# The rows of attention scores spread to all partitions through DRAM instead of by products of ones with diagonals

## The chip, the cores and the metric

The kernel runs on one core of one Trainium2 chip. The metric is the device time of one execution in microseconds (us); the time before is the median of three runs. A core has a matrix engine (TensorE, PE in the profile, with its weight loads listed apart as PEld), a vector engine (VectorE, DVE), a scalar engine that also evaluates functions (ScalarE, ACT), a general engine that here only issues DMAs (GpSimd, POOL), and SyncE (SP), which also issues DMAs. Each has its own queue of instructions.

## The reference

Four layers over a graph of 2708 nodes with 512 features, each of the form `x = x + layer(relu(layernorm(x)))`, all in float32. The first three multiply the features by a normalised adjacency matrix and by a weight. The change is in the fourth, cut to what matters:

```python
s_left, s_right = (x @ W_sa) @ a_left, (x @ W_sa) @ a_right
scores = s_left[:, None] + s_right[None, :]
e = where(adj != 0, exp(-leaky_relu(scores, 0.01)), 0)
attn = e / (sum(e, axis=1) + 1e-5)
x_a = attn @ (x @ W_sa)
x_b = adj @ (x @ W_gcnb) + b_gcnb
out = sigmoid(attn_a * x_a + attn_b * x_b)
```

`attn_a` and `attn_b` are gates: sigmoids of one number for each node. The kernel works on the transposed matrix: output nodes are columns, and the nodes that are summed over lie on partitions. So `s_right` is a bias for each partition, and `s_left` is a row that every partition must hold. The kernel divides numerator and denominator by a common factor for each output node, built from the least `s_right` (`srmin`). With m = max(s + srmin, 0.01 (s + srmin)), the two rows are a = m - s and b = m - 0.01 s, and exp(-leaky_relu) becomes the lesser of exp(a - s_right) and exp(b - 0.01 s_right).

## The kernel before

**Tiles.** The 2708 nodes are four quarters (`NQ`) of 677 (`Q`): five tiles of 128 (`KT`) and 37 over. The rests of the four quarters are put together in two tail tiles (tile 20 with 4 x 32, tile 21 with 4 x 5), so there are 22 tiles (`NT`). The 677 columns of a quarter are processed as two pieces of 339 (`U`, `W`), the last of which has one column too many.

**Order of the layers.** The matrix products of layers 0 to 2 and of the gate part of layer 3 are built from sub-products of quarters (L538). For layer 3, `aggregate` does outer products 1, 7, 2, 4, 6 and 5, then calls an epilogue for the first half of the tiles, does outer product 3, and calls the epilogue for the second half (tiles 10 to 21). Hooks put other work into it: `row_scales` hangs on outer product 6, reloads of `h` on 5 and 3.

**The gated epilogue** (`gated`). For each tile there are two halves. A half is a product of 128 x 257 in four steps, each two PE instructions (L200), in one of two banks that also hold the products `pl`, `pm` of the rows. ACT takes the gate from the last column (tanh, L1049), DVE adds the bias to the other 256 (L1058), ACT multiplies by the other gate (L1059), and POOL stores the tile to DRAM (L1060).

**The rows** (`column_rows`). For each quarter, DVE makes seven diagonal matrices from `s_left` (L969), PE multiplies them by ones, so that each partition holds the numbers side by side (L970: 14 instructions, since each float32 product is two), ACT copies them from the bank (L1096, L1101 to L1103), and DVE computes the rows a and b with eight operations (L1107 to L1110). Quarter 0's rows are made between the first four gated tiles of the second half and the others (`gated_and_ready`); those of quarter q+1 at the middle of quarter q (`u == 1`, `b == 0`). The places of the rows are the pool tags s1 and s2 for even quarters, s3 and s4 for odd ones; before the attention these hold operands of outer product 3.

**The attention loop** (from L1191). It runs over quarters, pieces and five blocks: four blocks of five tiles and one of tails. `e_step` works one block ahead: a load of the block of the adjacency matrix, ten exponentials on ACT with the row as input (L1119), and two DVE operations that take the lesser and mask it (L1123, L1124). PE then multiplies the block with `h` (L1202, 40 instructions for a full block), DVE sums it up, and one tile of the output is finished beside it (`attention`). At the end of a piece come the tails' products (L600, L605) and four copies of the sums.

**What sets the order.** Python's order of calls is a priority; a scheduler of the tile framework decides from it the order on every engine's queue when the program is built. Waits follow from the use of tiles, and a tile taken from a pool waits until the readers of the tile that had its place are done.

Of the kernel before, what the change touches and what calls it, by code (L numbers as in the profile page):

```python
# [8 lines left out]
FP = mybir.dt.float32  # L9
AF = mybir.ActivationFunctionType  # L10
ALU = mybir.AluOpType

P = 128
D = 512
NC = D // P
N = 2708
NQ = 4
Q = N // NQ
KT = Q // P
R0 = 32  # L20
R1 = Q - KT * P - R0
U = 2
W = (Q + 1) // U
NF = NQ * KT
NT = NF + 2
R1P = 8
G = NQ * R1P
PAD = R1P - R1
# [9 lines left out]
def gnn_kernel(  # L38
# [20 lines left out]
    nc = tc.nc  # L59

    const = ctx.enter_context(tc.tile_pool(name="const", bufs=1))
# [3 lines left out]
    upool = ctx.enter_context(tc.tile_pool(name="upool", bufs=1))  # L65
    ytp = ctx.enter_context(tc.tile_pool(name="ytp", bufs=1))
    small = ctx.enter_context(tc.tile_pool(name="small", bufs=2))
    dram = ctx.enter_context(tc.tile_pool(name="dram", bufs=1, space=bass.MemoryType.DRAM))
    ps_agg = ctx.enter_context(tc.tile_pool(name="ps_agg", bufs=5, space=bass.MemoryType.PSUM))
    ps_out = ctx.enter_context(tc.tile_pool(name="ps_out", bufs=2, space=bass.MemoryType.PSUM))  # L70
# [3 lines left out]
    ident = const.tile([P, P], FP, name="ident")  # L74
# [6 lines left out]
    for k in range(1, P // G):  # L81
# [6 lines left out]
    bab = const.tile([P, 2], FP, name="bab")  # L88
    nc.gpsimd.dma_start(bab[:, 0:1], ba.partition_broadcast(P))
    nc.gpsimd.dma_start(bab[:, 1:2], bb.partition_broadcast(P))  # L90
    deg = const.tile([P, NT], FP, name="deg")
    dinv = const.tile([P, NT], FP, name="dinv")
    dis = const.tile([P, NT], FP, name="dis")
    hd = const.tile([P, NT, 4], FP, name="hd")
    mv0 = const.tile([P, NT, 2], FP, name="mv0")
    ga = const.tile([P, NT, 2], FP, name="ga")
# [1 line left out]
    eps = const.tile([P, NT], FP, name="eps")  # L98
# [9 lines left out]
        for b in range(2)  # L108
        for u in range(U)
    }  # L110

    h = big.tile([P, NT, D], FP, name="h")

# [850 lines left out]
    def broadcast_columns(po, cs):  # L964

        for s, c in enumerate(cs):
            r = c.shape[0]
            dg = small.tile([P, P], FP, tag="diag", name="dg", bufs=2)
            nc.vector.tensor_scalar(dg[:r, :r], ident[:r, :r], c, None, ALU.mult)  # L969
            nc.tensor.matmul(  # L970
                po[:, s * P : s * P + r], ones[:r, :], dg[:r, :r], start=True, stop=True
            )
# [99 lines left out]
    srmin = const.tile([P, 1], FP, name="srmin")  # L1072

    def row_scales():

        mn = small.tile([P, 1], FP, tag="ge", name="mn")
        nc.vector.tensor_reduce(mn, hd[:, :, 1], mybir.AxisListType.X, ALU.min)
        po = ps_out.tile([P, D], FP, tag="out", name="pm")
        broadcast_columns(po, [mn[:, 0:1]])
        nc.vector.tensor_reduce(srmin, po[:, 0:P], mybir.AxisListType.X, ALU.min)  # L1080
        nc.vector.tensor_scalar(nsr[:, :, 0], hd[:, :, 1], -1.0, None, ALU.mult)
        nc.vector.tensor_scalar(nsr[:, :, 1], hd[:, :, 1], -0.01, None, ALU.mult)
        nc.vector.tensor_scalar(eps, hd[:, :, 0], srmin, None, ALU.add)
        nc.vector.scalar_tensor_tensor(eps, eps, 0.01, eps, ALU.mult, ALU.max)
        nc.scalar.activation(eps, eps, AF.Exp)
        nc.vector.tensor_scalar(eps, eps, 1e-5, None, ALU.mult)

    def column_rows(q):

        ra, rb = (  # L1090
            spool.tile([P, U * W], FP, tag=f"s{1 + k + 2 * (q % 2)}", name=f"r{k}") for k in (0, 1)
        )
        nc.vector.memset(ra[:, Q : U * W], 0.0)
        pl = ps_out.tile([P, D], FP, tag="out", name="pl")
        broadcast_columns(pl, [hd[:, q * KT + k, 0:1] for k in range(4)])
        nc.scalar.copy(ra[:, 0 : 4 * P], pl)  # L1096
        pl = ps_out.tile([P, D], FP, tag="out", name="pl")
        broadcast_columns(
            pl, [hd[:, q * KT + 4, 0:1], hd[:, NF, 0:1], hd[:G, NF + 1, 0:1]]
        )  # L1100
        nc.scalar.copy(ra[:, 4 * P : 5 * P], pl[:, 0:P])  # L1101
        nc.scalar.copy(ra[:, KT * P : KT * P + R0], pl[:, P + q * R0 : P + (q + 1) * R0])
        nc.scalar.copy(ra[:, KT * P + R0 : Q], pl[:, 2 * P + q * R1P + PAD : 2 * P + (q + 1) * R1P])  # L1103
        for u in range(U):
            a, b = ra[:, u * W : (u + 1) * W], rb[:, u * W : (u + 1) * W]
            lm = upool.tile([P, W], FP, tag="s", name="lm")
            nc.vector.tensor_scalar(lm, a, srmin, None, ALU.add)  # L1107
            nc.vector.scalar_tensor_tensor(lm, lm, 0.01, lm, ALU.mult, ALU.max)
            nc.vector.scalar_tensor_tensor(b, a, -0.01, lm, ALU.mult, ALU.add)
            nc.vector.tensor_sub(a, lm, a)  # L1110
        return ra, rb

    def scores(blk, ts, ra, rb):
# [62 lines left out]
    def gated_and_ready(ts):  # L1176

        nonlocal ready
        if ts[0] < half:
            return gated(ts)  # L1180
        gated(ts[:4])
        lines[0] = column_rows(0)
        gated(ts[4:])
        ready = e_step(*steps[0])
# [6 lines left out]
    for n, (q, u, b) in enumerate(steps):  # L1191
        cu = slice(u * W, (u + 1) * W)
        se = sums[:, (q % 2) * U * W : (q % 2 + 1) * U * W]
        if b == 0:
            pe = [ps_agg.tile([P, W], FP, tag="agg", name=f"pe{c}") for c in range(NC)]
            if u == 1 and q + 1 < NQ:
                lines[q + 1] = column_rows(q + 1)
# [10 lines left out]
        for t, a in now:  # L1208
            if t == 0:
                nc.vector.tensor_copy(se[:, cu], a)  # L1210
            else:
                r = G if t == NF + 1 else P
# [14 lines left out]
        elif todo:  # L1227
            t, se_t = todo.pop(0)
# [70 lines left out]
```

## Time and profile before

| | |
|---|---|
| median of three runs | 2099.44 us (2096.2 to 2100.52) |
| profiled execution, its own time | 2098.61 us |
| its span, first to last instruction | 2096.7 us |
| granted PE clock | 0.997 of full |
| busy: PE / DVE / ACT / POOL | 2054.8 / 1416.4 / 409.2 / 182.8 us |
| PE instructions of L970 for the rows (`pl`) | 56, from 1580.9 to 1901.9 us |
| gated epilogue of the second half begins | 1567.07 us |
| middles of quarters 0, 1, 2 | 1661.6, 1779.9, 1898.3 us |

A line of the groups names source line, engine, operation, output and inputs with shapes, count, then busy time and mean in ns, then idle time of the engine ahead of it and what ended it. A line of a timeline gives start, duration, engine, line and operation; a number in brackets is the idle time before it and its releaser. Times are from the start of the span. A busy sum counts each instruction with its whole duration, and neighbours overlap; how often one can follow the other is read from their starts.

### The profile page before, as it was taken

Reading aid. Unit: us, or ns where it says so; the run is one execution under the profiler, and the core shown is the slowest. Engines: PE = TensorE matmul, PEld = TensorE weight load, DVE = VectorE, ACT = ScalarE, POOL = GpSimd, SP = SyncE. Lnnn points to the kernel's source line nnn. Section 1 sums busy time; section 2 is a strip of 40 time slices with the busy share of each in tenths; the row PEclk is TensorE's granted clock in tenths of the full one; section 3 lists DMA queues with packets and bytes.
Section 4 is the critical chain, followed back from the end, with each engine's and each line's share of the span. In section 5 each row is a group of like instructions: output and inputs, shape, how many; then the busy total and the mean of one; then the engine's idle time right before and its main releaser. Section 6 shows DMA issues by size and latency. Waiting matters only on the chain.

```text
span 2096.7 us, 20100 instructions
## 1 busy us (share of the span) xinstructions
PE 2054.8 (98%) x7340; PEld 1279.6 (61%) x7340; DVE 1416.4 (68%) x2481; ACT 409.2 (20%) x833; POOL 182.8 (9%) x330
## 2 busy tenths in 40 slices
PE   5999999999999999999999999999999999999998
PEld 2566655656666554666665556666777666666665
DVE  4578877657767777766686889867538755666512
ACT  1430001130000011100002120000117533444411
POOL 0110111120000012000002120000001000000011
PEclk9999999999999999999999999999999999999999
DMA  9998594555545354654445574555451223233220
GB/s 368 302 373 260 188 342 171 188 190 170 175 154 186 126 189 136 242 174 161 166 145 175 195 244 164 169 166 183 153 176 59 101 99 117 81 103 102 90 74 26
DMA packets 79746, 360.86 MB, mean 172 GB/s; under 512 B 10668, under 2 KB 15660, under 8 KB 79520
## 3 DMA queue, kind: packets, MB, share of 16 engines
q1 hardware_dynamic: 50672, 245.43, 34.0%
q0 software_dynamic: 28976, 114.15, 16.8%
q8 instruction: 58, 0.95, 0.2%
q14 instruction: 40, 0.33, 0.0%
HBM read 294.61 MB, written 62.15 MB: 170 GB/s over the span
## 4 chain that ended last, share of the span: by engine, by line
PE 87%; DVE 6%; DMA 4%; issue 1%; ACT 1%; POOL 0%; SPq 0%; POOLq 0%; DVEq 0%; ACTq 0%
PE pe L1202 17%; PE po L200 15%; PE pc L538 14%; PE pd L538 14%; PE pa L538 13%; PE pb L538 7%; PE pt L600 3%; DMA obuf<-in_yb_dram 2%; DMA ends<-in_yt_dram 1%; PE pt L605 1%; PE pe L600 1%; DVE ends L1001 1%; DMA ends<-xs 1%; PE dg_ps L321 1%; DVE t L511 0%
## 5 line engine op out<-in xcount | busy, mean ns | idle before, releaser
L1202 PE MATMUL pe<-obuf,h 128*128 128x339 f32 x1280 | 373.2, 448 | 0.0
L200 PE MATMUL po<-ends,agg 128*128 128x512 f32 (+2 forms) x968 | 352.1, 521 | 1.3 <-DVE ends L1058 1.0
L538 PE MATMUL pa<-obuf,h 128*128 128x339 f32 x1040 | 317.1, 449 | 2.5 <-ACT h L252 1.4
L1202 PEld LDWEIGHTS pe<-obuf,h 128*128 128x128 f32 x1280 | 240.8, 189 | 127.1 <-issue 10.8
L200 PEld LDWEIGHTS po<-ends,agg 128*128 128x128 f32 x968 | 181.3, 190 | 154.3 <-issue 137.4
L538 PEld LDWEIGHTS pa<-obuf,h 128*128 128x128 f32 x1040 | 195.6, 190 | 110.0 <-issue 9.8
L1119 ACT ACTIVATE e<-r,nsr 128x339 f32<-128x339 f32 x352 | 170.9, 565 | 25.0 <-DVE obuf L1123 11.5
L538 PE MATMUL pb<-t,s 128*128 128x339 f32 x560 | 171.2, 452 | 1.8 <-DVE s L470 1.0
L538 PE MATMUL pc<-t,h 128*128 128x339 f32 x560 | 169.5, 448 | 2.1 <-DVE u L585 2.1
L538 PE MATMUL pd<-t,s 128*128 128x339 f32 x560 | 169.0, 448 | 0.0
L538 PE MATMUL pd<-obuf,s 128*128 128x339 f32 x550 | 166.5, 448 | 1.3 <-DVE s L554 0.9
L572 ACT COPY v<-pa 128x339 f32<-128x339 f32 x56 | 24.6, 439 | 724.7 <-PE pa L538 698.8
L538 PEld LDWEIGHTS pb<-t,s 128*128 128x128 f32 x560 | 106.2, 190 | 57.2 <-DVE t L510 2.1
L538 PEld LDWEIGHTS pc<-t,h 128*128 128x128 f32 x560 | 105.7, 189 | 57.3 <-DVE u L585 3.6
L538 PEld LDWEIGHTS pd<-t,s 128*128 128x128 f32 x560 | 105.8, 189 | 54.1
L538 PEld LDWEIGHTS pd<-obuf,s 128*128 128x128 f32 x550 | 104.0, 189 | 55.2 <-DVE s L554 1.5
L538 PE MATMUL pc<-obuf,s 128*128 128x339 f32 x450 | 136.0, 448 | 0.0
L538 PEld LDWEIGHTS pc<-obuf,s 128*128 128x128 f32 x450 | 85.1, 189 | 43.8 <-issue 0.5
L510 DVE TENSOR_TENSOR t<-obuf,t 128x1695 f32<-128x1695 f32 x55 | 105.5, 1918 | 0.0
L932 POOL DMA_DIRECT2D xs<-ends x66 | 35.9, 544 | 782.4 <-DVE ends L931 706.8
L1219 DVE COPY agg<-pe 128x339 f32<-128x339 f32 x16 | 7.5, 507 | 137.0 <-PE pe L605 137.0
L578 DVE TENSOR_TENSOR u<-v,pb 128x339 f32<-128x339 f32 x56 | 28.4, 507 | 106.1 <-PE pb L538 106.0
(273 smaller groups left out, 2225.9 us busy)
## 6 DMA issues: line engine op xcount, KB each, us to landing
obuf<-in_yb_dram SPq DMA_DIRECT2D x132, 847.5 KB, 4.6
obuf<-osumt SPq DMA_DIRECT2D x100, 847.5 KB, 4.5
osumt<-obuf POOLq DMA_DIRECT2D x22, 847.5 KB, 12.2
xs<-ends POOLq DMA_DIRECT2D x66, 256.0 KB, 2.3
ends<-xs POOLq DMA_DIRECT2D x61, 256.0 KB, 3.9
obuf<-in_yt_dram SPq DMA_DIRECT2D x28, 339.0 KB, 3.5
obuf<-in_yb_dram POOLq DMA_DIRECT2D x11, 847.5 KB, 10.8
ends<-in_yb_dram SPq DMA_DIRECT2D x9, 847.5 KB, 9.5
```

Source lines behind the costliest of these rows:

```text
L200: nc.tensor.matmul(po, cs[c], ws[c], start=(c == 0), stop=(c == NC - 1))
L321: nc.tensor.matmul(ps[g], first, y, start=n < 4, stop=n >= len(ops) - 4)
L510: nc.vector.tensor_add(t2, o22, t1)
L538: last = nc.tensor.matmul(ps, x[:, k, :], y[:, k, :], start=start and k == 0, stop=k == KT - 1, skip_group_check=not start,)
L572: at_v.append(nc.scalar.copy(v, pa).ins)
L578: at_u2.append(nc.vector.tensor_add(u2, v, pb).ins)
L600: nc.tensor.matmul(ps[c], h[:, NF, c * P : (c + 1) * P], tl[:, 0, :], start=start, stop=False)
L605: nc.tensor.matmul(ps[c], h[g, NF + 1, c * P : (c + 1) * P], tl[g, 1, :], start=False, stop=True)
L932: nc.gpsimd.dma_start(xs[t], xt)
L1001: nc.vector.tensor_tensor_reduce(y, h[:, t, :], vs[:, k, :], 1.0, 0.0, ALU.mult, ALU.add, hd[:, t, k : k + 1])
L1119: nc.scalar.activation(e[:, k], row, AF.Exp, bias=nsr[:, t, s : s + 1], scale=1.0)
L1202: nc.tensor.matmul(pe[c], h[:, t, c * P : (c + 1) * P], a, start=(t == 0), stop=False)
```

## The change

The rows a and b are computed once for all nodes in `row_scales`, where the numbers lie as 128 x 22: two more DVE operations, which write into `dinv` and `dis` (no longer needed there). `deg`, `dinv` and `dis` become slices of one tile `dd`, so that one product with the identity turns both to 44 x 128. ACT copies that to a tile in SBUF, and 12 DMAs of POOL write it to a DRAM tile `ab_rows`, in the order of the columns (8 of five rows of 128, 2 for the tails of 32, 2 for those of 5). `column_rows` then only clears the last column of each row and loads it with one DMA from POOL's queue, which reads the 677 numbers for every partition (338.5 KB). The places where `column_rows` is called are as before.

```diff
-    deg = const.tile([P, NT], FP, name="deg")
-    dinv = const.tile([P, NT], FP, name="dinv")
-    dis = const.tile([P, NT], FP, name="dis")
+    dd = const.tile([P, 3, NT], FP, name="dd")
+    deg = dd[:, 0]
+    dinv = dd[:, 1]
+    dis = dd[:, 2]
...
+    ab_rows = dram.tile([NQ, 2, U * W], FP, name="ab_rows")
...
         nc.vector.scalar_tensor_tensor(eps, eps, 0.01, eps, ALU.mult, ALU.max)
+        nc.vector.tensor_sub(dinv, eps, hd[:, :, 0])
+        nc.vector.scalar_tensor_tensor(dis, hd[:, :, 0], -0.01, eps, ALU.mult, ALU.add)
         nc.scalar.activation(eps, eps, AF.Exp)
         nc.vector.tensor_scalar(eps, eps, 1e-5, None, ALU.mult)
+
+        po = ps_out.tile([P, D], FP, tag="out", name="pr")
+        nc.tensor.matmul(
+            po[: 2 * NT, 0:P], dd[:, 1:3].rearrange("p k t -> p (k t)"), ident,
+            start=True, stop=True,
+        )
+        r = small.tile([P, P], FP, tag="diag", name="rows", bufs=2)
+        nc.scalar.copy(r[: 2 * NT], po[: 2 * NT, 0:P])
+        for k in range(2):
+            for q in range(NQ):
+                t = k * NT + q * KT
+                nc.gpsimd.dma_start(
+                    ab_rows[q, k, 0 : KT * P].rearrange("(t p) -> t p", p=P), r[t : t + KT]
+                )
+            for o, t, m, c0 in ((KT * P, NF, R0, 0), (KT * P + R0, NF + 1, R1P, PAD)):
+                src = r[k * NT + t : k * NT + t + 1, 0 : NQ * m].rearrange(
+                    "o (q r) -> o q r", q=NQ
+                )
+                nc.gpsimd.dma_start(
+                    ab_rows[:, k, o : o + m - c0].rearrange("(o q) r -> o q r", o=1),
+                    src[:, :, c0:],
+                )
 
     def column_rows(q):
...
-        nc.vector.memset(ra[:, Q : U * W], 0.0)
-        pl = ps_out.tile([P, D], FP, tag="out", name="pl")
-        broadcast_columns(pl, [hd[:, q * KT + k, 0:1] for k in range(4)])
-        nc.scalar.copy(ra[:, 0 : 4 * P], pl)
-        pl = ps_out.tile([P, D], FP, tag="out", name="pl")
-        broadcast_columns(
-            pl, [hd[:, q * KT + 4, 0:1], hd[:, NF, 0:1], hd[:G, NF + 1, 0:1]]
-        )
-        nc.scalar.copy(ra[:, 4 * P : 5 * P], pl[:, 0:P])
-        nc.scalar.copy(ra[:, KT * P : KT * P + R0], pl[:, P + q * R0 : P + (q + 1) * R0])
-        nc.scalar.copy(ra[:, KT * P + R0 : Q], pl[:, 2 * P + q * R1P + PAD : 2 * P + (q + 1) * R1P])
-        for u in range(U):
-            a, b = ra[:, u * W : (u + 1) * W], rb[:, u * W : (u + 1) * W]
-            lm = upool.tile([P, W], FP, tag="s", name="lm")
-            nc.vector.tensor_scalar(lm, a, srmin, None, ALU.add)
-            nc.vector.scalar_tensor_tensor(lm, lm, 0.01, lm, ALU.mult, ALU.max)
-            nc.vector.scalar_tensor_tensor(b, a, -0.01, lm, ALU.mult, ALU.add)
-            nc.vector.tensor_sub(a, lm, a)
+        for k, r in enumerate((ra, rb)):
+            nc.vector.memset(r[:, Q : U * W], 0.0)
+            nc.gpsimd.dma_start(r[:, 0:Q], ab_rows[q, k, 0:Q].partition_broadcast(P))
         return ra, rb
```

## The prediction

> **What bounds the kernel now.** I read the page's busy times first, then the chain that ended last.
>
> ```profile
> PE 2054.8 (98%) x7340; PEld 1279.6 (61%) x7340; DVE 1416.4 (68%) x2481; ACT 409.2 (20%) x833; POOL 182.8 (9%) x330
> PE 87%; DVE 6%; DMA 4%; issue 1%; ACT 1%; POOL 0%; SPq 0%; POOLq 0%; DVEq 0%; ACTq 0%
> ```
>
> TensorE (PE) is busy 98% of the span and carries 87% of the chain. Work of VectorE (DVE) or ScalarE (ACT) that goes away is therefore worth nothing by itself; a product that PE need not do, or a wait of PE, is worth its time. The removed products `pl` (L970) are 56 PE instructions. So I went next to PE's timeline where they stand. At the middle of quarter 0, where the rows of quarter 1 are made:
>
> ```profile
> 1661.58 0.71 PE L970 MATMUL pl<-dg,ones 128*128 128x128 f32 x4
> 1662.13 0.73 PE L1202 MATMUL pe<-obuf,h 128*128 128x339 f32 x2
> 1662.84 0.71 PE L970 MATMUL pl<-dg,ones 128*128 128x128 f32 x4
> 1663.39 0.73 PE L1202 MATMUL pe<-obuf,h 128*128 128x339 f32 x2
> 1663.96 0.61 PE L970 MATMUL pl<-dg,ones 128*128 128x128 f32 x4
> 1664.41 0.73 PE L1202 MATMUL pe<-obuf,h 128*128 128x339 f32 x2
> 1665.07 0.40 PE L970 MATMUL pl<-dg,ones 32*128 32x32 f32 x2
> 1665.41 0.84 PE L1202 MATMUL pe<-obuf,h 128*128 128x339 f32 x2
> ```
>
> From 1661.58 to 1665.41 are 3.83 us, and only six of the block's products stand in them. Ten of those follow each other in 2.86 us elsewhere (1555.64 to 1558.50 in this timeline), 0.286 each, so six need 1.72. The rows cost PE 3.83 - 1.72 = 2.11 us here, gaps included. The same stretch comes again at 1779.94 to 1783.77 and 1898.29 to 1902.12. Quarter 3's middle, at 2016.7, has no rows to make, and PE goes from the tails to the next block without a gap there.
>
> Quarter 0's rows are made inside the gated stretch (lines of PE, then of ACT, then of DVE in the same timeline):
>
> ```profile
> 1567.07 14.04 PE L200 MATMUL po<-ends,agg 128*128 128x257 f32 x64
> 1580.94 0.61 PE L970 MATMUL pl<-dg,ones 128*128 128x128 f32 x4
> 1581.71 2.29 PE L970 MATMUL pl<-dg,ones 128*128 128x128 f32 x10 [0.16 <-DVE dg L969]
> ...
> 1569.00 0.26 ACT L1049 ACTIVATE ga<-po,hd 128x1 f32<-128x1 f32 x1 [18.44 <-PE po L200]
> 1569.30 0.42 DVE L1058 TENSOR_TENSOR ends<-po,ends 128x256 f32<-128x256 f32 x1 [0.97 <-ACT ga L1049]
> ```
>
> PE gives them 3.19 us (1580.73, where the first can start, to 1583.92, where the next gated product does). The windows (span, then busy time and instructions of PE, PEld, DVE, ACT) say how near the others are to a limit after that:
>
> ```profile
> 1584.00:1600.00 16.00, 14.99 (x68) 12.55 (x69) 13.55 (x25) 14.39 (x37) 1.62 (x3) 1.00 0.17 66
> 1600.00:1616.00 16.00, 15.98 (x72) 12.12 (x70) 15.83 (x31) 12.69 (x30) 1.62 (x3) 1.00 0.13 51
> 1661.60:1780.00 118.40, 118.40 (x421) 74.24 (x417) 67.95 (x114) 50.80 (x106) 8.06 (x15) 1.00 0.30 99
> ```
>
> Between 1584 and 1616 DVE and ACT are nearly full and PE waits for them: 1.0 us at 1593.9, and 1.3 us in four small waits up to 1616.7. From 1661 on, PE alone is full; DVE is at 57% and ACT at 43%.
>
> **What the Trainium skill says.** "DMA: Bandwidth & Descriptors", section "Anatomy of one DMA — SWDGE (gpsimd) path", prices a transfer from POOL's queue at 2.0 us plus its bytes over 436e3 per us: for a row of 677 numbers spread to 128 partitions (346,624 bytes) an estimate of 2.8 us. The trace's own broadcasts are dearer, so I use them. "PSUM — Partial Sum Buffer", section "Engine vs sequencer instructions", calls the queues of ACT, DVE and POOL strict FIFO: what stands behind a waiting instruction waits too. The trace agrees: PE's wait of 1.01 us at 1593.9 ends with DVE's L1058, an addition of 0.4 us that stood behind the score operation L1123 of 1.93 us begun at 1591.42.
>
> **The change, part by part.** (1) *Rows of quarters 1 to 3.* No product, diagonal or ACT copy is left; DVE issues two memsets and POOL two loads. The loads' buffers are last read a quarter earlier, and the rows are needed about 100 us later, so they are hidden, even at the dearest landing below. DVE's and ACT's savings are hidden behind PE too. PE gains 3 x 2.11 = 6.33 us.
>
> (2) *Preparation, about 1438.* One product (44 x 128) is added beside the existing `pm`, which costs PE 0.22 (1438.10 to 1438.32). I take 0.22. Two small DVE operations, 0.3 us together, stand where PE has other products. The 12 writes go to POOL's queue between 1442 and 1494, where it is idle, and are read 100 us later. If all were exposed they would cost a few us; the idle queue excludes it.
>
> (3) *Quarter 0's rows and the first block of scores.* This is the risk. In the built program's order the ten exponentials of the first block now stand on ACT **before** the first tanh of the second gated half (L1049), and the score operation (L1123) stands on DVE before the first gated addition (L1058). Before, four gated tiles went first. So the first addition now waits for a DMA. The row lands in a buffer that the last-but-one product `pd` of piece 3 reads until 1561.35:
>
> ```profile
> 1562.01 0.06 DVE L1093 MEMSET r<- 128x1 f32 x1
> ...
> ends<-in_bg_dram POOLq DMA_DIRECT2D x1, 256.0 KB, 4.1
> ends<-in_asa_dram POOLq DMA_DIRECT2D x2, 256.0 KB, 5.8
> L1119 ACT ACTIVATE e<-r,nsr 128x339 f32<-128x339 f32 x352 | 170.9, 565 | 25.0 <-DVE obuf L1123 11.5
> ```
>
> DVE can set the row's last column about 1562.0, POOL issue at 1562.4. The page's POOL broadcasts of 256 KB land in 3.6 to 4.1 us, and one `asa` took 8.3 (median of two 5.8) beside other transfers. Here five reloads of `h` run at 1563 to 1566.5, so I take 4.6: the row is there at 1567.0. (Bounds: 3.3, the fastest broadcast, and 8.3.) Nine exponentials at a pitch of 0.47 reach 1571.3; the score operation takes 1.93, to 1573.3; the first gated addition 0.38. Only two banks hold gated products, and each half takes PE 1.74 us, so the third could start at 1567.07 + 3.47 = 1570.54; it now starts at about 1573.8. **A new wait of 3.3 us.**
>
> What is late next? Up to tile 20 DVE has, in order, 12 score operations on five tiles (1.84 each: 22.1), 4 on tails (1.8), 20 gated additions (0.38: 7.6), 10 gate operations (0.7) and 22 column sums (0.42: 9.2): 41.4 us, from 1571.4 to 1612.8. PE has 20 halves (34.7) and 28 products of scores (8.0): 42.7 us, from 1567.07 plus 3.3 to 1613.1. DVE just keeps pace; the wait is paid once. I leave 1.3 us for the small waits about tiles 20 and 21. The stretch lost 3.19 + 2.3 = 5.5 us of PE before and loses 3.3 + 1.3 = 4.6 now: a gain of 0.9.
>
> (4) SP's order is the same. On POOL the four row loads stand before the second half's first store, none of which is due before they are issued.
>
> Sum: -6.33 + 0.22 - 0.9 = **-7.0 us**. The profiled execution's own time is 2098.61 (span 2096.7 and 1.9 around it), which becomes 2091.6. The median of the runs is 2099.44, 0.8 above it: **2092.4**.
>
> **Rivals.** *A row that lands late.* Beside the reloads, and with another row's load issued just before it, it could take the 8.3 us of the slower `asa`. Everything in (3) is later by 3.7 us: -7.0 + 3.7 = -3.3, 2096.1. Against it: most broadcasts landed in 4.1.
>
> *The first wait does not show.* If the row lands in 3.3, and DVE then catches up within the slack that PE's order leaves, two thirds of the wait and half of the small ones go: -7.0 - 2.9 = -9.9, 2089.5. Against it: even then nine exponentials and a score operation (6 us) stand ahead of the first addition.
>
> *VectorE becomes the bound: slower.* The margin of PE over DVE up to tile 20 is 42.7 - 41.4 = 1.3 us. If DVE's chain through ACT (tanh, then addition, behind exponentials) adds a wait to each half, PE loses it each time, as at 1593.9. At 0.6 us for each of 22 halves, 13.2 us: -7.0 + 13.2 = +6.2, 2105.6. It decides from 0.32 us for each half (no gain left) and passes 0.2% from 0.51. For it: the windows with DVE at 15.83 of 16. Against it: those windows held the same interleaved work, with PE at 15.98.
>
> *The rows still cost PE.* If PE's gaps at the quarters' middles came from DVE's queue (copies of `pe` and sums) and not from `pl`, most of the 6.33 would stay, and the time would be about 2098. Quarter 3's gapless middle speaks against it.
>
> **How the numbers follow.** Likeliest 0.62 (its own range 2089.5 to 2095: 2.5 to 3 us for the landing's bounds and the small waits); late row 0.16; no wait 0.10; DVE bound 0.09; rows still cost 0.03. What a measurement here can tell from no change is 0.2%, 4.2 us: faster is below 2095.2, slower above 2103.6. The likeliest case nearly whole, the no-wait case and a quarter of the late row give 0.74 faster; the rest of the late row, the rows that still cost and a few hundredths of the likeliest give 0.17 the same; 0.09 slower. The range of 8 in 10, 2087.5 to 2097.5, holds the likeliest, most of the late row and of the no-wait case.
>
> **What would show it.** Right: PE without a gap for 6 us after each tails' end at the quarters' middles; no `pl`; one `pr` of 0.22; a PE gap of some 3 us after the first 16 gated products of 1567, ended by DVE's L1058, with ACT's first exponential just after the row's landing near 1567 and ahead of the tanh. Wrong: a landing after 1569, a chain of gaps of 0.5 us or more between all gated halves, or a wait of SP or ACT on a row at a quarter's middle.

## The result, and the profile after

The changed kernel took 2091.23 us (median of 6 runs, 2087.98 to 2093.06) beside 2098.92 for the kernel before: a ratio of 0.9969 with a 95% interval of 0.9958 to 0.9980. Repeated with 21 runs (e5 below), it was 2092.10 beside 2096.68, 0.9979 (0.9972 to 0.9987). The medians lie 7.7 and 4.6 us apart; by the ratios, which are used for all gains below, the change gains 6.5 us (4.2 to 8.8) and 4.4 us (2.7 to 5.9). Forecast were 2092.4 and a gain of 7.0.

Busy times and the chain of the changed kernel's profile:

```profile
span 2087.6 us, 19939 instructions
PE 2044.6 (98%) x7286; PEld 1272.0 (61%) x7286; DVE 1397.4 (67%) x2427; ACT 404.5 (19%) x818; POOL 193.8 (9%) x350
PE 86%; DVE 6%; DMA 4%; issue 3%; ACT 0%; POOL 0%; SPq 0%; POOLq 0%; DVEq 0%; ACTq 0%
```

PE is the bound as before, with 54 instructions less: 56 of `pl` gone, two of `pr` new. The span is 9.1 us shorter than in the profile before, which is more than the change brought: `pm`, ahead of everything that the change touches, starts at 1435.44 in place of 1438.10. In the profiles of this study it starts anywhere from 1432.8 to 1440.5, also in one program (1434.0 to 1440.2), since the first 1400 us differ between executions. So I compare from `pm` on, up to the end of quarter 3's tails.

| stage, us | before | changed | e5, same program | e10, same program |
|---|---|---|---|---|
| `pm` to the start of the second half's gated stretch | 128.97 | 129.64 | 129.35 | 130.55 |
| gated stretch to the middle of quarter 0 | 94.51 | 93.08 | 94.90 | 93.60 |
| middle of quarter 0 to 1 | 118.36 | 116.25 | 116.24 | 116.25 |
| 1 to 2 | 118.35 | 116.24 | 116.25 | 116.25 |
| 2 to 3 | 118.36 | 116.26 | 116.25 | 116.25 |
| 3 to the tails' end | 56.29 | 56.29 | 56.29 | 56.29 |
| sum | 634.84 | 627.76 | 629.28 | 629.19 |
| against before | | -7.08 | -5.56 | -5.65 |
| from there to the end of the span | 23.81 | 24.40 | 24.39 | 24.41 |
| against before, with the end | | -6.49 | -4.98 | -5.05 |

Two rows need a word. In e10's first stage PE waits 1.56 us for DVE in the tails near 1481.5, where it waits 0.68 in the changed kernel's first profile. And the end of the program is 0.6 us longer in all three executions. The last store lands 21.7 to 21.8 us after quarter 3's tails in each of them and before, so this is not the stores: what stands behind that landing took 2.09 us before and 2.64 to 2.65 now, and the DRAIN that stands behind POOL's last store ends 1.00 us after the landing before and 1.86 to 1.87 after it now. Over the profiles of this study that end grows with the number of DMAs issued by POOL: 1.00 us for 319, 1.41 for 333 (e2), 1.74 for 337 (e1), 1.86 to 1.87 for 339, and 2.52 for 347 (e11). No run tests why.

The added product in PE's timeline, of which more below:

```profile
1435.67 3.03 PE L541 MATMUL pa<-obuf,h 128*128 128x339 f32 x10
1438.62 0.42 PE L1094 MATMUL pr<-ident,dd 128*44 128x128 f32 x2
1438.97 3.13 PE L541 MATMUL pb<-t,s 128*128 128x339 f32 x10
```

The middles. PE's timeline after, where quarter 1's rows had been made:

```profile
1657.38 0.85 PE L608 MATMUL pe<-tl,h 32*128 32x339 f32 x8
1658.16 5.12 PE L1214 MATMUL pe<-obuf,h 128*128 128x339 f32 x17
```

The tails are followed at once by the next block. Each middle is 2.10 to 2.11 us shorter. The rows' own DMAs (bytes each, median us to landing) are far ahead of their use there:

```profile
r<-ab_rows POOLq DMA_DIRECT2D x8, 338.5 KB, 3.7
ab_rows<-rows POOLq DMA_DIRECT2D x8, 2.5 KB, 3.0
```

The gated stretch, in the timelines of PE, POOL, ACT and DVE:

```profile
1565.08 3.63 PE L203 MATMUL po<-ends,agg 128*128 128x257 f32 x16
1570.79 2.00 PE L203 MATMUL po<-ends,agg 128*128 128x257 f32 x8 [2.09 <-DVE ends L1061]
...
1559.82 0.54 POOL L1122 DMA_DIRECT2D r<-ab_rows  x1 [2.31 <-PE pd L541]
1564.12 4.79 ACT L1131 ACTIVATE e<-r,nsr 128x339 f32<-128x339 f32 x10 [15.56 <-DMA r<-ab_rows]
1568.82 0.24 ACT L1052 ACTIVATE ga<-po,hd 128x1 f32<-128x1 f32 x1
1568.48 1.93 DVE L1135 SCALAR_TENSOR_TENSOR obuf<-obuf,e 128x1695 f32<-128x1695 f32 x1 [2.15 <-ACT e L1131]
1570.32 0.42 DVE L1061 TENSOR_TENSOR ends<-po,ends 128x256 f32<-128x256 f32 x1
```

The chain is the forecast one, link by link: the load waits for `pd`, lands 4.2 us after its issue, ten exponentials go ahead of the tanh, the score operation ahead of the first gated addition, and PE stops after 16 instructions, which are two halves. The windows (span; busy time of PE, PEld, DVE, ACT and POOL; PE's clock last but two) then show DVE fuller than before (13.55 and 15.83 us of 16 there), and PE full:

```profile
1582.00:1598.00 16.00, 16.00 (x73) 13.36 (x72) 15.86 (x33) 13.12 (x32) 1.79 (x4) 1.00 0.17 64
1598.00:1614.00 16.00, 16.00 (x69) 12.41 (x67) 15.86 (x30) 16.00 (x39) 2.00 (x4) 1.00 0.18 67
1658.20:1774.40 116.20, 116.20 (x406) 72.69 (x402) 63.61 (x100) 49.91 (x102) 9.16 (x17) 1.00 0.33 107
```

DVE keeps pace, and its 67.95 us of a quarter are 63.61 now, which PE doesn't notice.

### The profile page after: what moved, and what is told of

Its sections match the earlier page's. It is cut to its first block, busy times and chain, and to the rows that moved or that the text cites. A ratio compares the mean times of both kernels' runs of the same rounds, so it can differ in the third digit from the quotient of the medians.

```text
span 2087.6 us, 19939 instructions
## 1 busy us (share of the span) xinstructions
PE 2044.6 (98%) x7286; PEld 1272.0 (61%) x7286; DVE 1397.4 (67%) x2427; ACT 404.5 (19%) x818; POOL 193.8 (9%) x350
## 4 chain that ended last, share of the span: by engine, by line
PE 86%; DVE 6%; DMA 4%; issue 3%; ACT 0%; POOL 0%; SPq 0%; POOLq 0%; DVEq 0%; ACTq 0%
PE pe L1214 18%; PE po L203 15%; PE pc L541 13%; PE pa L541 13%; PE pd L541 13%; PE pb L541 7%; PE pt L603 3%; DMA obuf<-in_yb_dram 3%; PE pt L608 1%; PE pe L603 1%; DVE ends L1004 1%; DMA ends<-xs 1%; PE dg_ps L324 1%; DVE t L514 0%; DVE t L513 0%
## 5 line engine op out<-in xcount | busy, mean ns | idle before, releaser
L1131 ACT ACTIVATE e<-r,nsr 128x339 f32<-128x339 f32 x352 | 171.2, 567 | 47.8 <-DVE tl L1135 15.9
L513 DVE TENSOR_TENSOR t<-obuf,t 128x1695 f32<-128x1695 f32 x55 | 105.3, 1914 | 0.0
L514 DVE TENSOR_TENSOR t<-obuf,t 128x1695 f32<-128x1695 f32 x52 | 99.5, 1914 | 0.1
```

Of the source, the lines that this page charges most:

```text
L513: nc.vector.tensor_add(t2, o22, t1)
L514: at_y.append(nc.vector.tensor_add(t4, o21, t2).ins)
L1131: nc.scalar.activation(e[:, k], row, AF.Exp, bias=nsr[:, t, s : s + 1], scale=1.0)
```

## The experiments

My theory: 2.11 us at each of three middles are PE's own work for the rows and the waits within it; the added product takes a little back; the gated stretch trades 3.2 us of products for a wait behind the row's landing and what is queued with it. Rivals: the gain lies in the gated stretch; the middles' loss was waiting and not PE's work; the new wait is the landing alone; VectorE's sum sets the stretch's pace.

### Each part alone: e1 and e2

Both keep the old `column_rows` beside the new one, as `product_rows`.

```diff
 e1:
-        lines[0] = column_rows(0)
+        lines[0] = product_rows(0)
 e2:
-                lines[q + 1] = column_rows(q + 1)
+                lines[q + 1] = product_rows(q + 1)
```

> Rows of quarters 1 to 3 through DRAM, quarter 0's by products of ones with diagonals as in the kernel before. Theory (the gain lies at the three middles, 2.11 us each, and the added product takes back some 0.6): -5.7 us against the kernel before, each middle without a gap, and the gated stretch of the second half with its 3.2 us of products and no wait of 2 us after 16 products. Rival (the gain lies in the gated stretch): about -1 us or no change.

Measured: 2093.53 beside 2097.81, 0.9976 (0.9967 to 0.9986), that is -5.0 us (-6.9 to -2.9). By stages: 2.10 to 2.11 less at each middle, 94.46 in the gated stretch (94.51 before), 0.5 more in the first stage: -5.86 up to the tails' end, for 5.7 expected.

> Only quarter 0's rows through DRAM, those of quarters 1 to 3 by products. The instructions of the gated stretch stand as in the changed kernel. Theory: about -0.8 us against the kernel before (1.4 gained in the stretch, 0.6 lost at the added product), which a timing can't tell from nothing; the trace shows the wait of some 2.1 us behind the row's landing, and 2.11 us lost at each middle. Rival (the gain lies in the gated stretch): -6 us or more.

Measured: 2098.68 beside 2097.81, 1.0006 (0.9997 to 1.0015): no change. By stages: middles as before (58.42 and 59.94 for their pieces, as in the kernel before), 93.22 in the gated stretch with a wait of 2.22, -0.63 in all. So nearly all of the gain is at the middles, and the rival that puts it into the gated stretch falls.

### Is it PE's own work at the middles? e3

```diff
                 lines[q + 1] = column_rows(q + 1)
+                for n_cols in (4, 3):
+                    po = ps_out.tile([P, D], FP, tag="out", name="pl")
+                    for k in range(n_cols):
+                        nc.tensor.matmul(
+                            po[:, k * P : (k + 1) * P], ones, ident, start=True, stop=True
+                        )
```

> The changed kernel, with seven products of ones with the identity (14 PE instructions of 128 columns) put back at each of the three middles; nothing makes diagonals for them and nobody reads them. Theory (the products' own PE time was most of what was lost, 0.11 us an instruction as at pm): +1.5 us at each middle, 4.6 in all over the changed kernel, 3 below the kernel before. Rival (the loss was PE waiting for diagonals and for ACT's copies): less than 0.5 us a middle, time as the changed kernel.

Measured: 2096.03 beside 2097.81, 0.9992 (0.9984 to 1.0000). In the timeline of PE at the first middle:

```profile
1663.51 1.83 PE L1213 MATMUL pl<-ident,ones 128*128 128x128 f32 x14
1665.17 3.02 PE L1220 MATMUL pe<-obuf,h 128*128 128x339 f32 x10
```

The 14 instructions take 1.66 us here, with the step to the next; each of the three half quarters that begin with them is 1.56 us longer than in the changed kernel (57.85 to 57.87 for 56.29 to 56.30). So of 2.11 us, 1.56 were PE's own work; the theory's price of 1.5 was right.

The other 0.55 was put to waits for diagonals and copies, and the trace of the kernel before bears this out for the smaller part only. About 0.25 of it stands where the second group of `pl` begins. PE's weight load waits there for the diagonal that DVE makes:

```profile
1662.84 0.52 PEld L970 LDWEIGHTS pl<-dg,ones 128*128 128x128 f32 x4 [0.52 <-DVE dg L969]
```

About 0.30 stands around the last product, which has 32 rows and 32 columns, and which e3 replaced by a full one. By the starts that the prediction shows, two products of the block before it take 0.66 us where 0.57 is usual (1664.41 to 1665.07), its own two instructions 0.34, and the next product 0.1 more than usual: 0.52 in all, where two full instructions take 0.22. Its diagonal was finished 0.3 us before it began, so this is no wait for it; what it is, no run tells.

The timing's gain is 1.7 us, not 3. Part of it may lie in the gated stretch, which the experiment doesn't touch: in this profile it took 95.05 us and not 93.08, of which more below. But the profiled execution, with 2099.4 us, is slower than the median, so this is not shown for the others.

### What the wait in the gated stretch is worth: e4 and e8

```diff
-    def column_rows(q):
+    def column_rows(q, behind=None):
...
             nc.vector.memset(r[:, Q : U * W], 0.0)
+            if behind is not None:
+                nc.vector.tensor_copy(r[:, 0:1], behind)
             nc.gpsimd.dma_start(r[:, 0:Q], ab_rows[q, k, 0:Q].partition_broadcast(P))
...
-        lines[0] = column_rows(0)
+        lines[0] = column_rows(0, ga[:, ts[1], 0:1])
```

In e8 it is `ts[2]`. The load must wait until the column has been written, so the scheduler too puts the exponentials later.

> The changed kernel, with the load of quarter 0's rows held until the gate of the second tile of the second half is there (one column is written from the gate first), so that two or three tiles' tanh stand ahead of the exponentials. Theory A (the wait of 2.1 us after 16 products is a net loss): it goes, and nothing takes its place: 2 us below the changed kernel. Theory B (VectorE's sum up to tile 20 sets the pace, and a start of its score operations that is later by some us is paid further on): same time as the changed kernel or up to 2 us above it, with PE waits moved to later gated tiles.

> As e4_row_held, held behind the gate of the third tile, so the first exponentials stand 3.5 us later still, about where the kernel before has them. Theory A (a late start of the scores is free until VectorE's margin of some 1 to 3 us is used): the stretch takes 92 us or a little more, as with two tiles. Theory B (it is paid in full): 3 us more than e4_row_held, 95.

Measured: e4 2090.35 beside 2097.81, 0.9962 (0.9947 to 0.9977); e8 2089.62 beside 2096.68, 0.9962 (0.9948 to 0.9976). The gated stretch takes 92.01 and 91.93 us, 1.1 less than the changed kernel's best and 3 less than e5's. PE's timeline of e4:

```profile
1567.58 14.04 PE L203 MATMUL po<-ends,agg 128*128 128x257 f32 x64
1582.43 2.00 PE L203 MATMUL po<-ends,agg 128*128 128x257 f32 x8 [0.82 <-DVE ends L1061]
1584.62 3.71 PE L203 MATMUL po<-ends,agg 128*128 128x257 f32 x16 [0.19 <-DVE ends L1061]
1588.61 1.97 PE L203 MATMUL po<-ends,agg 128*128 128x257 f32 x8 [0.28 <-ACT e L1133]
```

No wait stands after 16 instructions, three short ones stand where the scores begin, and the exponentials begin 12.5 us into the stretch (15.9 in e8), where the changed kernel has them 1.0 ahead of it. For e4 neither account is quite right: half of the 2.1 us comes back as later waits. For e8 the first account came true, since the later start was not paid at all. So VectorE's sum doesn't set the pace in full. That both are faster than the changed kernel is read from the stages; by the timings they can't be told from it.

### One program, two gated stretches: e5 and e10

These are the changed kernel again, e10 for one execution (2089.40 us).

> The changed kernel once more, beside the three below. Theory: 6.4 us below the kernel before by the stages after the added product (0.65 lost there, 1.43 gained in the gated stretch, 2.11 at each middle, up to 0.6 lost at the end of the program); what more the first comparison showed came from before the change, in the first 1435 us, and should not come back.

> The changed kernel a third time, for one more look at the clock after PE's wait of 2.1 to 2.4 us at the start of the gated stretch. Theory (whether the clock falls differs between executions of one program): a gated stretch of either 93 us with the clock at 1.00 after the wait, or 95 us with 0.50 to 0.8 for 3 to 5 us. Rival (it is fixed by the length of the wait): the clock falls if the wait is over 2.3 us and not otherwise.

The gain ahead of `pm` did not come back, as expected: e5's `pm` starts at 1440.2. But its gated stretch is 94.90 us. PE's timeline after its wait:

```profile
1569.56 3.63 PE L203 MATMUL po<-ends,agg 128*128 128x257 f32 x16
1575.51 2.76 PE L203 MATMUL po<-ends,agg 128*128 128x257 f32 x8 [2.31 <-DVE ends L1061]
1578.06 1.34 PE L1214 MATMUL pe<-obuf,h 128*128 128x339 f32 x2
1579.19 5.78 PE L203 MATMUL po<-ends,agg 128*128 128x257 f32 x24
```

From the end of the wait these 34 instructions take 9.3 us, and 7.7 in the changed kernel's first profile: 1.6 us more. In that profile and in e10, whose wait is longer, the clock is 1.00 throughout:

```profile
1564.59 3.63 PE L203 MATMUL po<-ends,agg 128*128 128x257 f32 x16
1570.82 2.00 PE L203 MATMUL po<-ends,agg 128*128 128x257 f32 x8 [2.60 <-DVE ends L1061]
```

So the wait's length doesn't decide it. The traces show what does. In each of them all changes of the granted clock lie whole multiples of 3.413 us apart, to within 4 ns, so that the profile can be cut into stretches of that length. Here are the stretches around the wait, three of e5 and then three of the changed kernel's first profile (span; busy time of PE; clock last but two):

```profile
1573.19:1576.61 3.42, 1.11 (x6) 0.99 (x6) 3.42 (x3) 3.42 (x9) 0.00 (x0) 1.00 0.30 120
1576.61:1580.02 3.41, 3.41 (x9) 2.43 (x8) 2.71 (x6) 2.78 (x8) 0.09 (x1) 0.50 0.00 0
1580.02:1583.43 3.41, 3.41 (x17) 2.97 (x16) 2.98 (x5) 2.92 (x8) 0.46 (x1) 1.00 0.20 77
1565.56:1568.97 3.41, 3.14 (x15) 2.40 (x13) 1.24 (x4) 3.41 (x10) 0.51 (x1) 1.00 0.77 261
1568.97:1572.38 3.41, 1.59 (x7) 1.43 (x8) 3.41 (x3) 3.41 (x9) 0.00 (x0) 1.00 0.23 95
1572.38:1575.80 3.42, 3.42 (x16) 2.68 (x16) 3.38 (x7) 3.42 (x10) 0.55 (x1) 1.00 0.07 28
```

In e5 the whole wait falls into one stretch, and the next stretch runs at half the clock. In the other profile the wait is divided between two. Sorted by the longest idle time of PE within one stretch, the waits of this part of the program read:

| run | wait, us | of it in one stretch | clock in the next |
|---|---|---|---|
| e5 | 2.31 | 2.31 | 0.50 |
| e6 | 2.08 | 2.08 | 0.50 |
| e3 | 2.45 | 2.01 | 0.50 |
| e9 | 1.86 | 1.86 | 0.50 |
| changed, first profile | 2.09 | 1.82 | 1.00 |
| e7 (in outer product 3) | 1.81 | 1.81 | 1.00 |
| e10 | 2.60 | 1.64 | 1.00 |
| e2 | 2.22 | 1.56 | 1.00 |

The same holds in all 13 profiles from 150 us to 15 us before the end. Twelve stretches at full clock hold 1.86 to 2.57 us of idle time of PE, and each is followed by one at 0.50; the other 7297 hold 1.84 or less, and none is. In the first 150 us, where PE has products of a single column that count as busy (122.4 to 124.9 us in the changed kernel's first profile), the clock also falls after stretches without idle time.

"TensorE: Matmul & The Clock Gate" of the Trainium skill says in its part 1, "The HAM clock gate", that activity is watched in windows of about 3.4 us that run freely, that the clock has two states, half and full, and that it falls after at least one idle window. The windows and the two states agree with these traces. The last point doesn't, as the window need not be idle: 1.86 us of 3.41 sufficed.

### The rows sooner: e6, e7, e9 and e11

All load quarter 0's rows into places that come free sooner. e6 only swaps places:

```diff
-            spool.tile([P, U * W], FP, tag=f"s{1 + k + 2 * (q % 2)}", name=f"r{k}") for k in (0, 1)
+            spool.tile([P, U * W], FP, tag=f"s{t}", name=f"r{k}")
+            for k, t in enumerate((1, 4) if q % 2 else (2, 3))
```

> The changed kernel with other places for the rows: quarter 0's in those that come free at 1551 and 1557 (s2 and s3) in place of s1 and s2, so both rows land some 3 us sooner. In the built order 21 exponentials then stand ahead of the first tanh, in place of 10. Theory (the wait is what stands ahead of the first tanh and of the first gated addition on their queues): exponentials from 1561, 21 of 0.47 us, first tanh after 1571, PE's wait 3 us or more in place of 2.1. Rival (the wait is the landing of the row alone): no wait.

Measured: 2091.93 beside 2096.68, 0.9978 (0.9968 to 0.9988), no gain over the changed kernel. ACT's timeline:

```profile
1553.09 2.45 ACT L1132 ACTIVATE e<-r,nsr 128x339 f32<-128x339 f32 x5 [7.32 <-DMA r<-ab_rows]
1560.67 7.60 ACT L1132 ACTIVATE e<-r,nsr 128x339 f32<-128x339 f32 x16 [5.13 <-DMA r<-ab_rows]
1568.18 0.24 ACT L1052 ACTIVATE ga<-po,hd 128x1 f32<-128x1 f32 x1
```

Both rows are there by 1560.7 and PE, whose stretch starts at 1563.79, still waits 2.08 us: the queues ahead of the tanh and of the first addition, not the landing alone, make the wait. I had it longer (3 us): five of the 21 exponentials came before the second row. And a second wait of 1.24 us appears in outer product 3, behind the score operation on DVE; the clock fell as well, and the stretch took 95.75.

e7 adds two edits to the order: the five exponentials of one row first, and the second block behind the first tanh.

```diff
-        for k, t in enumerate(ts):
-            for e, row, s in ((e1, ra, 0), (e2, rb, 1)):
+        for e, row, s in ((e1, ra, 0), (e2, rb, 1)):
+            for k, t in enumerate(ts):
...
-        (now, blks), ready = ready, e_step(*steps[n + 1]) if n + 1 < len(steps) else None
+        behind = {0: 0}.get(n)
+        with nullcontext() if behind is None else tc.issue_after(tanhs[half + behind].ins):
+            nxt = e_step(*steps[n + 1]) if n + 1 < len(steps) else None
+        (now, blks), ready = ready, nxt
```

> As e6_rows_earlier, with the five exponentials of the first row ahead of the five of the second, and the second block's exponentials kept behind the tanh of the first tile. So the first block's scores are made before the gated stretch begins, where ScalarE and VectorE are idle. Theory: no wait after 16 products, VectorE has 3.7 us less to do up to tile 20, the stretch takes about 90.5 us in place of 93.1, the time is 2.5 us below the changed kernel and 9 below the kernel before. Rival (VectorE's chain through ScalarE sets the stretch's pace): waits of the same sum at later tiles, time as the changed kernel.

Measured: 2090.53 beside 2096.68, 0.9967 (0.9955 to 0.9980). The gated stretch is 89.90 us without a wait of PE, a little better than expected, but outer product 3 ahead of it lost 2.1. PE, then DVE:

```profile
1559.16 3.02 PE L541 MATMUL pd<-t,s 128*128 128x339 f32 x10
1563.99 3.12 PE L541 MATMUL pc<-t,h 128*128 128x339 f32 x10 [1.81 <-DVE r L1124]
1561.60 1.93 DVE L1138 SCALAR_TENSOR_TENSOR obuf<-obuf,e 128x1695 f32<-128x1695 f32 x1 [4.58 <-ACT e L1134]
1563.44 0.50 DVE L588 TENSOR_TENSOR u<-u,pc 128x339 f32<-128x339 f32 x1
```

DVE stood at its score operation, which waited for exponentials, while the addition u (L588) that frees PE's bank was behind it. The releaser that the line of PE names is the small memset right after that addition. e9 keeps the score operation behind that addition:

```diff
-        ready = e_step(*steps[0])
+        with tc.issue_after(at_u3[-1]):
+            ready = e_step(*steps[0])
```

> As e7_early_and_fenced, with VectorE's operations of the first block kept behind the addition (u) that outer product 3 needs last, since there PE waited 1.81 us. Theory: that wait goes, outer product 3 takes 74.97 us again, the gated stretch stays at 90 us: 3 us below the changed kernel's better executions, some 4 to 5 below those in which the granted clock falls, 9 to 10 below the kernel before. Rival (the score operations that stand among outer product 3's own additions hold up another product): the wait shows up at the next product of outer product 3, time as e7.

Measured: 2092.28 beside 2099.95, 0.9963 (0.9951 to 0.9975). Outer product 3 takes 74.97 us again, the gated stretch 93.33: the wait went to the first gated addition, 1.86 us, and the clock fell after it. DVE's timeline names the cause:

```profile
1567.09 1.93 DVE L1139 TENSOR_TENSOR obuf<-obuf,e 128x1695 f32<-128x1695 f32 x1 [3.06 <-ACT e L1134]
...
1572.67 0.42 DVE L1063 TENSOR_TENSOR ends<-po,ends 128x256 f32<-128x256 f32 x1
```

The second row landed at 1564.5 only, so the second score operation ended at 1569.0, and ten of DVE's operations stood between it and the gated addition. e11 therefore makes a place hold both rows of one piece, so that both needed rows land early:

```diff
-            spool.tile([P, U * W], FP, tag=f"s{t}", name=f"r{k}")
+            r = spool.tile([P, 2, W], FP, tag=f"s{t}", name=f"r{u}")
...
+                nc.gpsimd.dma_start(
+                    r[:, k, 0:n], ab_rows[q, k, u * W : u * W + n].partition_broadcast(P)
+                )
...
-        ra, rb = (a[:, cu] for a in lines[q])
+        ra, rb = (lines[q][u][:, k] for k in range(2))
```

> As e9_early_past_u, with a place holding both rows of one piece in place of one row of both pieces. So all that the first block needs fits in the place that comes free at about 1551 to 1553 us, and both rows land before 1560 in place of one at 1558.7 and one at 1564.6. Theory (in e9 the second row's late landing put VectorE's second score operation and the additions queued behind it ahead of the first gated addition): both score operations are done by 1566, no wait after 16 products and no fall of the clock; outer product 3 at 75.0 us, the gated stretch at 90; 3 to 5 us below the changed kernel, 9 to 11 below the kernel before. Rival (VectorE's queue at the start of the stretch is what counts, whatever the landing): a wait of over 1 us after 16 products stays.

Measured: 2089.07 beside 2097.33, 0.9963 (0.9949 to 0.9977), that is -7.8 us (-10.7 to -4.8). In the trace outer product 3 takes 74.97 and the gated stretch 89.90 us. PE and DVE:

```profile
1564.66 9.21 PE L203 MATMUL po<-ends,agg 128*128 128x257 f32 x40
1562.33 1.93 DVE L1143 TENSOR_TENSOR obuf<-obuf,e 128x1695 f32<-128x1695 f32 x1 [1.55 <-ACT e L1138]
```

Both score operations are over before the gated stretch starts, and nothing waits in it. From `pm` to the tails' end it takes 624.33 us: 10.5 below the kernel before, 3.4 to 5.0 below the changed kernel. The end of the program, with eight DMAs more on POOL's queue, takes 25.06 us, which leaves 9.3 and 2.8 to 4.3. By the timings its lead over the changed kernel is within their intervals (0.9963 against 0.9969 and 0.9979); the stages show it.

## Why the prediction was right

The mechanism was right link by link, and so was the sum from `pm` to the tails' end (-7.0 forecast; -7.08, -5.56 and -5.65 measured). That the time agrees so closely (2092.4 forecast; 2091.23 and 2092.10 measured) is in part luck: it was counted from 2099.44 us, and in the repeat the kernel before took 2096.68. The steps:

- *Rows of quarters 1 to 3*: -6.33 forecast, -6.32 in the trace, and e1 shows the gain is there. e3 adds what the sum did not separate: three quarters of it is PE's own work.
- *The added product*: 0.22 forecast, mis-sized. By `pr` PE is 0.55 us later at the same place in the tails that follow (43.93 us after `pm`, for 43.38), and alike in e1, e2 and all others. `pr` starts 0.35 us before the next product, and the groups of ten on both sides take 2.95 and 2.96 where 2.86 is usual. The price was taken from `pm`, a full product. The weights of `pr` have only 44 columns, and it costs about what the small last product of the removed rows cost, 0.52 with what stands around it. No run tried small products by themselves.
- *The new wait*: 3.3 forecast; 2.09, 2.31 and 2.60 in three executions. The term that was too large is the row's landing. I put the memset ahead of the load, but POOL's load waited for `pd` itself and was issued 0.46 us after its end, not 1.05; the exponentials began 0.96 us ahead of the gated stretch, where I had 0.07. The landing took 4.2, where I had 4.6.
- *The small waits of the gated stretch*: 1.3 forecast. By difference they are about 2.0 in the changed kernel's first profile, an estimate: the stretch before, 94.51, less the 5.5 that the prediction counts as lost there, leaves 89.0 for PE's work, and 93.08 less that and the wait of 2.09 leaves 2.0. This takes back part of what the shorter wait gave.
- *VectorE just keeps pace*: right. No chain of waits followed; the stretch gained 1.43 in the first profile and 0.91 in e10, where I had 0.9.
- *What was missing*: the clock and the end of the program. A wait of two microseconds that falls into one stretch of 3.41 us cost PE another 1.6 in e5, which ate the stretch's gain and 0.4 more. The end of the program costs 0.6. The sum held although it left both out, because other errors stood against them; in e5 and e10 it is 1.4 us too large without the end and 2.0 with it.

Of the rivals, the late row (8.3 us) did not come: in the changed kernel's first profile no row took more than 5.1, and in e10 one that is needed later took 6.4. VectorE as the bound did not come either; e4 and e8 show why, since it has room for scores that start 13 to 17 us later. The first wait did not hide. That the rows still cost PE is excluded by the middles.

## What to carry to other kernels

Where TensorE is full, small products in the middle of its stream cost their own time, waits for what feeds them, and more where one is smaller than the engine: here 1.56, 0.25 and 0.30 us for seven products of at most 128 columns. A row that was known long before came by DMA without a wait of PE wherever its place was free early. It was not free of cost elsewhere: one more product in the preparation and a longer end of the program took back 0.55 and 0.6 us. Where a load makes work possible sooner, look at what now stands behind that work on each queue: score operations held up the gated stretch (2.1 us), then an outer product (1.8 us), until both their inputs came early enough. Where a wait of TensorE seems to cost more in one execution than in another, cut the profile at the changes of the granted clock and see how the wait lies.

## What the runs showed of the hardware

In each profile the changes of TensorE's granted clock lay whole multiples of 3.413 us apart. From 150 us to 15 us before the end it fell to 0.50 for a stretch of that length after each of twelve stretches with 1.86 to 2.57 us of idle time of PE, and after none of 7297 with 1.84 or less; in e5 this cost 1.6 us. The ends of PE's instructions are modelled in the profile, and no run varied the wait on purpose.

The first 1435 us of the program, which no kernel here changes, ended anywhere within 8 us (1432.8 to 1440.5), which is as much as the change is worth: only comparisons by stage could tell the parts. Much of this goes with the clock: between 23 us and `pm` there was no stretch at half clock in e6, which is earliest, and there were two in the changed kernel's first profile and e10 (1435.4 and 1434.0), four in e1 (1440.5) and five in e5 (1440.2). Over the 13 profiles the correlation is 0.87, at 1.6 us a stretch; no run tested it.

A row of 338.5 KB, read from DRAM for all partitions, landed 3.4 to 6.4 us after its issue in all profiles.
